# One position of the second convolution filtered along columns, a two-chunk map between the convolutions, and inner column sums in pairs

## The chip, the cores and the metric

The kernel runs on one core of a Trainium2 chip. The metric is the device time of one launch, in microseconds. Engines are named as in the profile: PE multiplies matrices (its weight loads are PEld), DVE, ACT and POOL work on vectors, SP and POOL issue DMAs. "L1482" is line 1482 of the kernel before.

## The reference

Four layers on an image batch x of 4 x 256 x 56 x 56 in float32, each with a group norm in front and a residual around it:

```python
x = x + involution_7x7(gn(x), ...)            # layer 0
x = x + basic_block(gn(x), w1, ..., w2, ...)  # layer 1: the one that changes
x = x + involution_7x7_bn(gn(x), ...)         # layer 2
x = x + fourier_gate(gn(x), W, b)             # layer 3

def basic_block(x, w1, ..., w2, ...):
    h = relu(bn1(conv3x3(x, w1)))
    return relu(x + bn2(conv3x3(h, w2)))      # 256 channels in and out
```

## The kernel before

**Layer 1 as a whole.** `conv_layer` (L1183) holds both convolutions. An image is cut into three chunks of rows, so that there are 12 chunks over the 4 images: for the first convolution `C1_ROWS` (20, 18 and 18 rows), for the second `C2_ROWS` (16, 20 and 20 rows). The list `order` (L1682) alternates them: first convolution of chunk 0, then, for i from 1 to 11, first convolution of chunk i and second convolution of chunk i-1, and last the second convolution of chunk 11. One entry of `order` is called a step here.

**Six positions.** Each row of 56 pixels is 14 tiles of four. `transform` (L1382, DVE) turns the 3-tap filtering along a row into six positions k, in the order `KS = (1, 2, 3, 4, 0, 5)`; `row_weights` and `summed_weights` make six weight planes of them for each of the three filter rows. For one position, PE multiplies 128 x 128 weight blocks with columns of n*14 pixels, n being the rows of the chunk, and DVE and ACT join the six products to four output pixels.

**Two ways to do a position.** `unfiltered` (L1478) takes the three filter rows as they are: for each of two output halves, two input halves times three filter rows, so 12 matmuls of n*14 columns, all on L1482. The filtered way, which stands inside `conv1` (L1510 to L1537), also filters along columns: it takes pairs of rows, and does with four products what six did. That is 16 matmuls of n/2*14 columns, on L1520. It needs prepared inputs: two inner sums (L1464, L1465, on DVE) and an outer difference v[y]-v[y+2]. The difference is two instructions (L1457 and L1458): ACT writes the negated lower rows, and a POOL DMA adds the upper rows onto it. In chunk 1 alone DVE makes it (L1455). It also needs prepared weights (`column_weights`, `filter_weights`) and more joining: ACT copies the first inner product (L1529), DVE forms its difference and sum with the second (L1533, L1534) and adds the outer products (L1536). The first convolution uses the filtered way in all six positions from chunk 2 on, in five in chunk 1 and in none in chunk 0. The second convolution uses `unfiltered` everywhere.

**A matmul in float32 is two records** of PE in this profile, each with its own weight load: a step with 72 unfiltered matmuls shows 144 records.

**Order of the work around them.** Program order on each engine is written out by hand. Each step has lists `after[0]` to `after[11]`, two for each position, that `run_all` empties at fixed points between the matmuls; they hold the transforms of the chunks to come, the column sums (`columns`, L1443), the scaled input rows (`phases`, L1363), loads, and what the step before left over (`tail1`, `tail2`, `late_r`). PSUM is four buffers of two banks: a filtered position takes two buffers, an unfiltered one takes one, so that PE must wait when DVE or ACT has not read the products from two filtered positions ago.

**The map between the convolutions.** `ph2` holds a whole image of the first convolution's result, 58 rows with the edges; `input2` transforms from it 18, 20 and 20 new rows for the three chunks, and copies two known rows for the second and third.

**The end of a second-convolution chunk.** Position 0 and position 5 are done by output half: position 0 half 0, position 5 half 0, position 0 half 1, position 5 half 1 (L1656 to L1670), with `joined` after each half. In the last two chunks `joined` adds the residual on DVE (L1611, L1616), from one shared buffer `res` that ACT fills (L1587); in the others ACT writes (L1603) and a POOL DMA accumulates the residual.

Of the kernel before, what the change touches and what calls it, by code (L numbers as in the profile page):

```python
# [16 lines left out]
P = 128  # L17
# [38 lines left out]
C1_ROWS = [(0, 20), (20, 38), (38, 56)]  # L56
# [16 lines left out]
def net_kernel(  # L73
# [1109 lines left out]
    def conv_layer(xin, xout, st, ahead):  # L1183
        with ExitStack() as es:
# [51 lines left out]
            v2_sb = wpool.tile([P, 2 * NY], F32, name="v2_sb")  # L1236

            def new_v2(half):

                n_v2[half] += 1  # L1240
                at = (n_v2[half] - 1) % 4
                if half:
                    return [room["v2"][:, at * NY : (at + 1) * NY]]
                if at == 3:
                    return [room[r][:, 5 * NY : 5 * NY + NY // 2] for r in ("v2", "xr")]
                t = room["v2"][:, 4 * NY : 5 * NY] if at == 2 else v2_sb[:, at * NY : (at + 1) * NY]
                return [t[:, : NY // 2], t[:, NY // 2 :]]
# [63 lines left out]
            def column_weights(ci, k0, k1):  # L1311

                w0, w1, w2 = (u1_sb[:, ci, y, k0:k1, :] for y in range(3))
                x = between_weights(ci, k0, k1)
                s = y_tile(5 if k0 == 5 else 3)[:, : (k1 - k0) * C].rearrange("p (k n) -> p k n", n=C)
                tt(s, w0, w2, ALU.add)
                tt(x, s, w1, ALU.subtract)
                tt(w1, s, w1, ALU.add)


            PL, VP = (0, 2, 1, 3), (0, 1, 2, 3, 5, 4)
            ph1 = wpool.tile([P, 4, CV_ROWS + 2, NB, WT + 1], F32, name="ph1")
            ph2 = wpool.tile([P, 4, H + 2, NB, WT + 1], F32, name="ph2")
# [3 lines left out]
            for j in range(4):  # L1327
                for y in (0, H + 1):
                    nc.gpsimd.memset(ph2[:, j, y], 0.0)
# [33 lines left out]
            def phases(i):  # L1363

                y0, y1, lo, hi = rows1(i)
                n, r0, known = y1 - y0 + 2, lo - (y0 - 1), 2 if i % 3 else 0
# [5 lines left out]
                for ci in range(NB):  # L1372
                    at = ci * (CV_ROWS + 2) * W
                    xr = room["rows"][:, at + known * W : at + (hi - lo) * W].rearrange("p (r t j) -> p j r t", t=WT, j=4)
                    for j in range(4):
                        q, t0 = (j + 1) % 4, (j + 1) // 4
                        dst = ph1[:, PL[q], r0 + known : r0 + hi - lo, ci, t0 : t0 + WT]
# [4 lines left out]
            def transform(v, ph, y0, n, known):  # L1382

                if known is not None:
                    old, m = known
                    nc.scalar.copy(
                        v[:, :, : 2 * NB].rearrange("p k r t -> p k (r t)"),
                        old[:, :, m * NB : (m + 2) * NB].rearrange("p k r t -> p k (r t)"),
                    )
                    v, y0, n = v[:, :, 2 * NB :], y0 + 2, n - 2  # L1390
# [36 lines left out]
            v_sb = [wpool.tile([P, WPOS, (CV_ROWS + 2) * NB, WT], F32, name=f"v{k}") for k in range(2)]  # L1427

            def input1(i):
                y0, y1, _, _ = rows1(i)  # L1430
                v = v_of[1, i] = v_sb[min(i, 1)]
                p0, p1 = C1_ROWS[i % 3 - 1]
                known = (v_of[1, i - 1], p1 - p0) if i % 3 else None
                yield from transform(v, ph1, 0, y1 - y0 + 2, known)

            def input2(i):
                y0, y1 = C2_ROWS[i % 3]
                v = v_of[2, i] = v_sb[i == n_chunks - 1]
                p0, p1 = C2_ROWS[i % 3 - 1]
                known = (v_of[2, i - 1], p1 - p0) if i % 3 else None  # L1440
                yield from transform(v, ph2, y0, y1 - y0 + 2, known)

            def columns(i, k, half):  # L1443

                y0, y1, _, _ = rows1(i)
                n = y1 - y0
                m = n // 2
                v = v_of[1, i][:, VP[k]]
                if half:
                    (t,) = new_v2(1)  # L1450
                    v = v.rearrange("p r t -> p (r t)")
                    at = slice(0, n * NB * WT)
                    below = slice(2 * NB * WT, (n + 2) * NB * WT)
                    if i == 1:
                        tt(t[:, at], v[:, at], v[:, below], ALU.subtract)  # L1455
                    else:
                        nc.scalar.mul(t[:, at], v[:, below], -1.0)  # L1457
                        nc.gpsimd.dma_start(t[:, at], v[:, at], accum_op=ALU.add)  # L1458
                    t = t.rearrange("p (r e n) -> p e r n", e=2, n=NB * WT)
                    v2_of[i, k, 1] = [t[:, e] for e in range(2)]  # L1460
                else:
                    v = v.rearrange("p (r e c) t -> p e r (c t)", e=2, c=NB)
                    t = v2_of[i, k, 0] = [x.rearrange("p (r n) -> p r n", n=NB * WT) for x in new_v2(0)]
                    tt(t[0][:, :m], v[:, 1, :m], v[:, 0, 1 : m + 1], ALU.add)  # L1464
                    tt(t[1][:, :m], v[:, 0, 1 : m + 1], v[:, 1, :m], ALU.subtract)  # L1465


            FIRST = [(k, half) for k in KS[:4] for half in range(2)]
# [16 lines left out]

            def conv1(i, after, tail):
# [3 lines left out]
                m = n // 2 * WT  # L1490
                a, t, b, s, q = (y_tile(k)[:, : NB * n * WT] for k in (0, 1, 2, 5, 4))
                first = s if i else q
                home = {1: s, 2: q, 3: t, 4: s, 0: y_tile(3)[:, : NB * n * WT], 5: s}

                def outputs(*js):
                    for j in js:
                        o = (a, t, b, q)[j].rearrange("p (c r t) -> p c r t", c=NB, t=WT)
                        p, t0 = PL[(j + 1) % 4], (j + 1) // 4
                        for co in range(NB):
                            nc.scalar.activation(  # L1500
                                ph2[:, p, y0 + 1 : y1 + 1, co, t0 : t0 + WT],
# [7 lines left out]
                for n_s, k in enumerate(KS):  # L1509
                    if k in filtered(i):  # L1510
                        va = v2_of[i, k, 0]
                        vb = v2_of[i, k, 1]
# [372 lines left out]
```

## Time and profile before

| | before |
|---|---|
| median of three runs | 1740.52 us (1738.83 to 1744.15) |
| the profiled execution, its own time | 1735.74 us |
| its span, first to last instruction | 1733.9 us |
| granted PE clock, mean over the span | 0.984 |
| PE busy, weight loads busy | 96%, 85% of the span |
| DVE, ACT, POOL busy | 76%, 54%, 27% of the span |
| layer 1 on PE, first to last convolution matmul | 517.9 to 1186.3 us |
| L1482, unfiltered | 1896 records, 422.8 us |
| L1520, filtered | 2080 records over all its groups |

The durations of single PE records overlap, since matmuls are pipelined: how long a matmul takes in a stream is read from the distance of the starts. A timeline row gives the start, the length, the engine, line and shape, the number of merged instructions, and in brackets the idle time before it with what ended it. A windows row gives, for one stretch, each engine's busy time with the number of instructions in brackets, then the granted clock, the DMA share and the data rate.

### The profile page before, as it was taken

What the parts mean: (1) busy time and instruction counts of PE and PEld (TensorE: products, weight loads), DVE (VectorE), ACT (ScalarE), POOL (GpSimd) and SP (SyncE); (2) the same over time, 40 slices, a digit from 0 to 9 for tenths busy, and PEclk for the clock granted to TensorE, in tenths of its full rate; (3) what the DMA queues carried; (4) which work ended last, traced back from release to release, by engine and by line L of the source; (5) the groups of instructions that cost most, each with busy time, mean ns of one, the idle gap of its engine ahead of it and who ended that gap; (6) DMA issues with size and microseconds to landing.
All of it is one profiled execution on the core that took longest, in us unless ns stands there. A gap on an engine that the chain in (4) does not pass through costs nothing.

```text
span 1733.9 us, 56359 instructions
## 1 busy us (share of the span) xinstructions
PE 1664.7 (96%) x24296; PEld 1479.3 (85%) x24296; DVE 1317.1 (76%) x2467; ACT 933.5 (54%) x2024; POOL 476.4 (27%) x669
## 2 busy tenths in 40 slices
PE   6999999999999999999999999998999899999998
PEld 4998998888977999898899889986988788788886
DVE  2777787777769887798878888856787678778775
ACT  2655556456646455443455245325667567577564
POOL 2223322323334111211122111100000563563571
PEclk9999999999989999999999999999999999999996
DMA  2455444543659546454565354553444666664652
GB/s 89 129 167 162 137 151 160 166 129 103 220 184 260 95 106 142 76 125 96 119 143 97 82 118 92 100 167 104 147 142 151 206 208 196 210 209 161 203 161 103
DMA packets 89030, 252.15 MB, mean 145 GB/s; under 512 B 14453, under 2 KB 35966, under 8 KB 85070
## 3 DMA queue, kind: packets, MB, share of 16 engines
q1 hardware_dynamic: 57438, 163.33, 29.1%
q0 software_dynamic: 30304, 83.95, 22.6%
q8 instruction: 192, 3.15, 0.8%
q10 hardware_dynamic: 1040, 1.26, 0.3%
q14 instruction: 56, 0.46, 0.1%
HBM read 95.07 MB, written 49.15 MB: 83 GB/s over the span
## 4 chain that ended last, share of the span: by engine, by line
PE 70%; DVE 15%; DMA 4%; ACT 4%; issue 3%; SPq 2%; POOL 2%; ACTq 0%; POOLq 0%; DVEq 0%
PE mm L1482 22%; PE ps L593 14%; PE ps L635 14%; PE mm L1520 11%; DVE kt L611 5%; PE ps L407 3%; DVE un L655 3%; DMA xw<-xw 2%; DMA u_sb<-in_wc_dram 2%; PE ps L469 2%; DVE st L1105 1%; ACT hp L488 1%; SPq L425 1%; ACT kt L604 1%; PE ps L718 1%
## 5 line engine op out<-in xcount | busy, mean ns | idle before, releaser
L1482 PE MATMUL mm<-v,u_sb 128*128 128x280 f32 (+2 forms) x1896 | 422.8, 384 | 0.7 <-DVE xs L1534 0.7
L1482 PEld LDWEIGHTS mm<-v,u_sb 128*128 128x128 f32 x1896 | 357.8, 189 | 62.2 <-issue 1.7
L635 PE MATMUL ps<-kt,xw 126*32 126x48 f32 (+1 forms) x12544 | 378.9, 235 | 20.9 <-issue 8.2
L635 PEld LDWEIGHTS ps<-kt,xw 126*32 126x32 f32 (+1 forms) x12544 | 340.6, 121 | 65.8 <-issue 41.5
L593 PE MATMUL ps<-hp,z_sb 64*126 64x133 f32 x6144 | 385.2, 279 | 9.2 <-DVE kt L611 5.0
L593 PEld LDWEIGHTS ps<-hp,z_sb 64*126 64x126 f32 x6144 | 365.1, 186 | 25.7 <-DVE kt L611 7.1
L611 DVE TENSOR_TENSOR kt<-ps,zb_sb 126x798 f32<-126x798 f32 x352 | 333.0, 980 | 59.4 <-PE ps L593 59.0
L604 ACT ACTIVATE kt<-ps,zb_sb 126x133 f32<-126x133 f32 x960 | 281.0, 442 | 108.4 <-PE ps L593 108.4
L655 DVE SCALAR_TENSOR_TENSOR un<-ps,s,un 128x240 f32<-128x240 f32 x224 | 102.4, 457 | 83.4 <-ACT un L650 79.3
L1520 PE MATMUL mm<-xs,u_sb 128*128 128x126 f32 (+1 forms) x1296 | 159.7, 277 | 4.4 <-DVE xs L1534 2.6
L655 DVE SCALAR_TENSOR_TENSOR un<-ps,par_sb,un 128x240 f32<-128x240 f32 x224 | 97.5, 456 | 82.0 <-ACT un L648 78.1
L1520 PEld LDWEIGHTS mm<-xs,u_sb 128*128 128x128 f32 x1296 | 153.3, 191 | 5.4 <-issue 2.9
L660 POOL TENSOR_TENSOR xs<-un,xs 128x240 f32<-128x240 f32 x112 | 72.1, 665 | 216.1 <-DVE un L655 216.1
L419 ACT COPY xw<-ps 126x896 f32<-126x896 f32 x112 | 101.4, 906 | 41.7 <-DMA xw<-xw 22.8
L1458 POOL DMA_DIRECT2D xs<-v x60 | 52.8, 1015 | 249.4 <-ACT xs L1457 248.5
L407 PE MATMUL ps<-ident_sb,strip_sb 128*126 128x128 f32 x784 | 111.6, 282 | 7.7 <-issue 4.3
L150 POOL TENSOR_TENSOR norm_sb<-norm_sb,mhalf 128x1 f32<-128x1 f32 x32 | 19.2, 601 | 360.5 <-DVE norm_sb L149 360.5
L648 ACT ACTIVATE un<-ps,par_sb 128x240 f32<-128x240 f32 x112 | 50.3, 449 | 119.4 <-PE ps L635 109.8
L650 ACT ACTIVATE un<-ps,bn_t,s 128x240 f32<-128x240 f32 x112 | 60.2, 538 | 88.2 <-PE ps L635 80.0
L407 PEld LDWEIGHTS ps<-ident_sb,strip_sb 128*126 128x126 f32 x784 | 84.2, 140 | 19.5 <-issue 5.4
L1603 ACT ACTIVATE xs<-hp,raw,raw 128x1120 f32<-128x1120 f32 (+1 forms) x20 | 45.2, 2260 | 97.7 <-DVE hp L1666 97.7
L1379 ACT ACTIVATE ph<-xs,norm_sb 128x294 f32<-128x294 f32 (+2 forms) x96 | 80.7, 865 | 9.5 <-DMA xs<-x 7.6
(291 smaller groups left out, 2010.0 us busy)
## 6 DMA issues: line engine op xcount, KB each, us to landing
xw<-xw SPq DMA_DIRECT2D x224, 252.0 KB
xw<-xw SPq DMA_DIRECT2D x224, 126.0 KB
xs<-x POOLq DMA_DIRECT2D x26, 560.0 KB, 5.9
x<-xs POOLq DMA_DIRECT2D x8, 1568.0 KB, 8.2
xs<-x SPq DMA_DIRECT2D x8, 1568.0 KB
xs<-v POOLq DMA_DIRECT2D x42, 252.0 KB, 4.2
xs<-in_x_dram SPq DMA_DIRECT2D x6, 1568.0 KB
x<-xs SPq DMA_DIRECT2D x6, 1568.0 KB
```

Source lines behind the costliest of these rows:

```text
L407: nc.tensor.transpose(ps[:Q, k * P : (k + 1) * P], flat[:, k * Q : (k + 1) * Q], ident_sb)
L419: nc.scalar.copy(xw[:, :NSB, :], ps[:Q, : NSB * P].rearrange("q (n c) -> q n c", n=NSB))
L593: nc.tensor.matmul(ps[:Q, i, k * NT : (k + 1) * NT], z_sb[i * R : (i + 1) * R, cb * GB // 2 + gp, z0 : z0 + Q], hp[i * R : (i + 1) * R, py ...
L604: nc.scalar.activation(kt[:, g0 + i, pb, :, k], ps[:Q, i, k * NT : (k + 1) * NT], AF.Identity, bias=zb_sb[:, cb * GB + g0 + i, p0 + k : p0 ...
L611: nc.vector.tensor_tensor(kt[:, g0 : g0 + 2, pb], ps[:Q, :, : PB * NT].rearrange("q i (k t) -> q i t k", k=PB), zb_sb[:, cb * GB + g0 : cb ...
L635: nc.tensor.matmul(v[m * j : m * j + m, i, :, k * TP : (k + 1) * TP], xw[:, window(ty), m * j : m * j + m], kt[:, ng * j : ng * j + ng, :, ...
L650: nc.scalar.activation(part, o[0], AF.Identity, bias=bn["t4"][:, cb : cb + 1], scale=bn["s4"][ng][:, 0, cb : cb + 1])
L655: nc.vector.scalar_tensor_tensor(part, o[e], s, part, ALU.mult, ALU.add)
L660: nc.gpsimd.tensor_tensor(dst, u, dst, ALU.add)
L1379: nc.scalar.activation(dst, xr[:, j], AF.Identity, bias=t, scale=s)
L1482: nc.tensor.matmul(ps, *position(u, v, ci, dy, k, co, n), start=(j == 0), stop=(j == NB * 3 - 1))
L1520: nc.tensor.matmul(ps[:, bank, co * m : (co + 1) * m], u[ci][:, co * P : (co + 1) * P], v2[e][:, : n // 2, ci * WT : (ci + 1) * WT], start ...
```

## The change

- **Row split.** The first convolution's chunks are 18, 20 and 18 rows. The second's stay.
- **Position 0 of the second convolution is filtered**, in all 12 chunks. A new function `filtered_product` holds what stood in `conv1`, and both convolutions call it. Its prepared weights (`column_weights2`, `filter_weights2`) are made during the second convolution's chunk 0. `conv2` now does five positions whole, in the order 1, 2, 3, 4, 0, and position 5 by output half.
- **Column sums.** `columns` becomes `inner_columns`, which makes the two inner sums of two positions in one pair of DVE instructions, and `outer_columns`. The pair (0, 5) of the first convolution is made at the head of its own step.
- **Map of two chunks.** `ph2` is two halves of 20 rows, used in turn. `input2` transforms 19, 20 and 19 new rows, and copies three known ones. POOL clears the one edge row of a chunk (`edge_rows`).
- **Buffers and places.** The inner sums of positions 1 and 2 lie in two planes of `ph1`, and `phases` of the next chunk therefore starts at `after[4]` and not at `after[1]`. The outer differences have five buffers. In the last two chunks each output half has its own residual buffer. The ACT and POOL part of the second half's `joined` moves into the next step, and its store one step later.

```diff
-C1_ROWS = [(0, 20), (20, 38), (38, 56)]
+C1_ROWS = [(0, 18), (18, 38), (38, 56)]
+PH_ROWS = 20
...
+            FILTERED2 = (0,)
+            ux2_sb = [wpool.tile([P, NB, C], F32, name=f"ux2_{k}") for k in FILTERED2]
+            def column_weights2(ci, k):
+                s = y_tile(5)[:, :C]
+                column_sums_of(*(u2_sb[:, ci, y, k, :] for y in range(3)), ux2_sb[FILTERED2.index(k)][:, ci], s)
...
-            ph2 = wpool.tile([P, 4, H + 2, NB, WT + 1], F32, name="ph2")
+            ph2 = wpool.tile([P, 4, 2 * PH_ROWS, NB, WT + 1], F32, name="ph2")
...
+            def inner_columns(conv, i, *ks):
+                n = rows_of(conv, i)
                 m = n // 2
...
+                t = t[:, : len(ks)].rearrange("p k e (r n) -> p k e r n", n=NB * WT)
+                tt(t[:, :, 0, :m], v[:, :, 1, :m], v[:, :, 0, 1 : m + 1], ALU.add)
+                tt(t[:, :, 1, :m], v[:, :, 0, 1 : m + 1], v[:, :, 1, :m], ALU.subtract)
+            def outer_columns(conv, i, k):
...
+                if (conv, i) == (1, 1):
+                    tt(t[:, at], v[:, at], v[:, below], ALU.subtract)
+                else:
+                    nc.scalar.mul(t[:, at], v[:, below], -1.0)
+                    nc.gpsimd.dma_start(t[:, at], v[:, at], accum_op=ALU.add)
...
-                res = ux_sb.rearrange("p c k n -> p (c k n)")[:, : n * W]
+                results = [u1_sb[:, co].rearrange("p y k n -> p (y k n)")[:, : n * W] for co in range(NB)]
...
+                        def leaves():
+                            nc.scalar.activation(x.rearrange("p (q j) -> p j q", j=4), y, AF.Identity, bias=t, scale=s)
+                            nc.gpsimd.dma_start(x, xin[bb][co][:, at], accum_op=ALU.add)
+                        if co == 0:
+                            leaves()
+                        else:
+                            late_r[0].append(leaves)
...
-                for n_s, k in enumerate(KS[:4]):
+                for n_s, k in enumerate(KS[:5]):
+                    if n_s == 4:
+                        residual(0)
+                    if k in filtered2(i):
+                        ux = [ux2_sb[FILTERED2.index(k)][:, ci] for ci in range(NB)]
+                        filtered_product(2, i, k, s, u2_sb, ux, after[2 * n_s])
+                        full, got = (lambda x: x), s
+                    else:
...
+                    else:
+                        stt(full(p), full(p), -0.75, got, ALU.mult, ALU.add)
+                        stt(p, r, 0.25, p, ALU.mult, ALU.add)
                     run_all(after[2 * n_s + 1])
-                residual(0)
+                residual(1)
                 for co in range(NB):
                     at = slice(co * m, (co + 1) * m)
                     ps = one_bank()[:, :m]
-                    unfiltered(ps, u2_sb, v, 0, co, n)
-                    stt(p[:, at], p[:, at], -0.75, ps, ALU.mult, ALU.add)
-                    stt(p[:, at], r[:, at], 0.25, p[:, at], ALU.mult, ALU.add)
-                    run_all(after[8 + 2 * co])
-                    ps = one_bank()[:, :m]
                     unfiltered(ps, u2_sb, v, 5, co, n)
...
+                    if i > 0:
+                        after[0].append(lambda i=i: (inner_columns(1, i, 0, 5), outer_columns(1, i, 0)))
+                        if i > 1:
+                            after[2].append(lambda i=i: outer_columns(1, i, 5))
...
-                            place(after, phases(i + 1), range(1, 10))
+                            place(after, phases(i + 1), range(4, 12))
...
+                    if filtered2(i):
+                        after[2].append(lambda i=i: inner_columns(2, i, *filtered2(i)))
+                        for n, k in enumerate(filtered2(i)):
+                            after[2 + n].append(lambda i=i, k=k: outer_columns(2, i, k))
...
-                        for n, (k, half) in enumerate(FIRST):
-                            after[(5, 5, 6, 6, 7, 7, 8, 8)[n]].append(lambda j=j, k=k, half=half: columns(j, k, half))
+                        columns_at(after, (6, 8), ((4, 1), (4, 2), (6, 3), (9, 4)), 1, j)
```

## Prediction

> **What bounds the kernel now.** First the page's busy shares, then the two stretches of layer 1 in the windows view:
>
> ```profile
> PE 1664.7 (96%) x24296; PEld 1479.3 (85%) x24296; DVE 1317.1 (76%) x2467; ACT 933.5 (54%) x2024; POOL 476.4 (27%) x669
> ```
> ```profile
> 517.90:575.30 57.40, 53.36 (x307) 45.86 (x306) 54.05 (x95) 35.01 (x60) 21.46 (x18) 0.99 1.14 242
> 575.30:1186.30 611.00, 608.90 (x3700) 553.05 (x3698) 498.70 (x901) 259.79 (x375) 95.23 (x111) 1.00 0.50 108
> ```
>
> From 575 us to 1186 us PE is busy 608.9 of 611.0 us at full clock. Who kept it waiting there is the whole answer of the waits view for PE (wait in total, times, longest):
>
> ```profile
> PE mm L1520 <- DVE xs L1534: 1.1, 2, 0.5
> PE mm L1482 <- DVE xs L1534: 0.7, 3, 0.2
> ```
>
> So PE bounds this stretch, and a PE microsecond saved is an end moved, as long as the others keep up. The first 57 us are different: DVE is busy 54.05 of 57.40 us, more than PE, and PE waits for it 4.1 us.
>
> What a matmul costs in a stream I read from the starts in PE's timeline:
>
> ```profile
> 663.29 1.12 PE L1520 MATMUL mm<-xs,u_sb 128*128 128x140 f32 x8
> ...
> 686.17 34.12 PE L1482 MATMUL mm<-v,u_sb 128*128 128x280 f32 x144
> 720.13 1.05 PE L1520 MATMUL mm<-v_sb,u_sb 128*128 128x126 f32 x8
> ...
> 741.57 27.41 PE L1482 MATMUL mm<-v,u_sb 128*128 128x224 f32 x144
> 768.81 1.05 PE L1520 MATMUL mm<-xs,u_sb 128*128 128x126 f32 x8
> ```
>
> Per record: 280 columns (720.13-686.17)/144 = 235.8 ns; 224 columns (768.81-741.57)/144 = 189.2 ns; 140 columns (686.17-663.29)/192 = 119.2 ns; 126 columns (741.57-720.13)/192 = 111.7 ns. The 252-column records take 5.10/24 = 212.5 ns (575.33 to 580.43).
>
> DVE's timeline shows how near the 16-row second-convolution step (741.57 to 768.81 on PE) is to a DVE bound:
>
> ```profile
> 752.86 0.61 DVE L1645 TENSOR_TENSOR hp<-hp,mm 128x448 f32<-128x448 f32 x1
> ...
> 761.51 0.61 DVE L1650 TENSOR_TENSOR hp<-hp,mm 128x448 f32<-128x448 f32 x1
> ```
>
> Four positions of 24 records (4.54 us) put the second product on PE at 750.65 and the fourth at 759.73: DVE reads them 2.2 and 1.8 us late, and works from 741.24 to 767.5 almost without a gap.
>
> [...] 140 columns follow the slope of the longer ones ((235.8-189.2)/56 = 0.83 ns a column), 126 columns lie 4 ns above it. [...] The trace has 0.68 us for 504 and 0.41 for 252, so merging two into one saves. [...] The DMA list of the page has 4.2 us median for this very accumulation; the measurement is used.
>
> **The change, part by part.**
>
> *Position 0 filtered.* 24 records of n*14 columns become 32 of half as many. 20 rows: 24 x 235.8 = 5.66 us against 32 x 119.2 = 3.81 us, 1.85 us saved, in 8 chunks 14.8 us. 16 rows: 24 x 189.2 = 4.54 us against 32 records of 112 columns, which the trace doesn't show. By the slope they would take 96 ns (saving 1.47 us), by the 126-column row[...] 111.7 ns (saving 0.97 us). I take the floor because 126 columns already sit on it: 4 x 0.97 = 3.9 us, upper end 5.9. Sum **-18.7 us**.
>
> *What it adds on DVE*, per 16-row step, in start-to-start time: inner sums 2 x 0.31; joining 0.38 + 0.38 + 0.57; position 0 in two whole instructions (1.2) for four halves (1.5); the four pairs of 252 (8 x 0.33) become two pairs of 504 (4 x 0.60), -0.25; 19 transformed rows for 18, +0.2. Together +1.6 us. DVE needed some 26.2 us of 27.2; now 27.8 us of 26.3. It ends that step 1.5 us behind, perhaps 2. Does PE feel it? Behind it comes a first-convolution step of 21.4 us in which DVE has 17.6 busy (windows view, 720.1 to 741.6), and PE needs a PSUM buffer only two positions after it filled it: the inner one is read some 1 us after the inner half (1.79 us) and due again at 7.14 us, over 3 us of slack. So **0**; if the cover is gone, 1.5 us in 4 steps. 20-row steps have 27.7 us of DVE busy in 33.9 us and go to about 29.2 in 32.1 (686.2 to 720.1).
>
> *ACT and POOL*: per chunk one negation (L1457, 0.62 us), one copy (0.38 us) and one DMA issue (0.87 us); ACT is busy 260 of 611 us, POOL 95. The difference is issued about 8 us into the step, behind the transform it reads, and lands 4 to 5 us later; PE needs it at 4 x 4.54 + 1.79 = 20 us (16 rows) or 24 us (20 rows). **0**. Behind the negation stand ACT's copies of positions 3 and 0, needed at 13.6 us at the earliest. The moved half of `joined` (ACT 2.0 to 2.5 us) now stands behind the first copy of the next step instead of in front; in the trace that copy made DVE wait 1.47 us (724.00) without a PE wait, so **0** again. Its POOL DMA comes ahead of the difference for position 0 of the first convolution, due 14 us later. Its store passes to SP behind the next row loads, which are needed a step later.
>
> *Row split and start.* Chunk 0 loses 144 x (235.8-212.5) = 3.4 us on PE, chunk 1 gains 160 x (119.2-111.7) + 24 x 23.3 ns = 1.7 us. Were PE the bound, -1.7 us. But this stretch is DVE's. Its work up to PE's last wait (566.3 us): chunk 0's transform -0.8, its joining 10 x -0.06 = -0.6, chunk 1's transform +0.7, column sums +0.9 (20 rows, and position 5's, which isn't used there): +0.2. It begins 0.4 us earlier, as ACT's eight `phases` have 19 rows for 21. Behind that wait PE still has 80 filtered records and 24 others, now longer by 80 x 7.5 + 24 x 23.3 ns = 1.2 us. A `phases` instruction of 0.7 us that stood ahead of ACT's copy there has moved to a later slot: -0.7. **+0.3 us**, bounds -1.7 and +2. The second convolution's chunk 0 also gets six DVE instructions of 0.42 us for the weights; it had 3.9 us of DVE gaps (580 to 608): 0. Later images have the same three sizes in another order: 0.
>
> *The tail.* The chain of waits from 1180 us:
>
> ```profile
> 1181.66 1.40 DVE ux_sb L1611
> 1183.08 2.20 DVE xs L1616
> 1185.31 2.41 ACT ux_sb L1587
> 1187.74 1.40 DVE ux_sb L1611
> 1189.16 2.29 DVE xs L1616
> ...
> 1191.74 0.84 POOL strip_sb L371
> ```
>
> Layer 2 starts behind the second L1616, 5.2 us after PE's end (1186.25). With two residual buffers ACT's 2.41 us leave this chain, but half 0 is now complete only 2.83 us before PE's end, not 5.66. DVE then runs (0.46 + 0.48 + 1.40 + 2.20) twice, with gaps 9.2 us, from 2.8 before the end to 6.4 after: **+1.2 us**, bounds 0 and 1.5.
>
> Sum: -18.7 + 0.3 + 1.2 = **-17.2 us**. The profiled execution took 1735.74 us, with 1733.9 of span: it becomes 1718.5. The median shown, 1740.52, lies 4.8 us above that execution; the same step from it gives **1723 us**.
>
> **The rivals.**
> - *DVE becomes the bound of the second-convolution steps.* For it: the lag of 2 us in the 16-row step. Against it: PSUM slack, and no PE wait above 0.5 us in 611. If the 4 x 1.5 us pass on and the 8 steps of 20 rows stall by half a us each: 1723 + 6 + 4 = 1733.
> - *PE gets all of it.* 112 columns stream at 96 ns (-2.0), the start follows PE (-2.0), the tail is hidden (-1.2): 1718.
> - *Slower: the outer difference lands late.* One place, the outer matmuls of position 0: the matmuls queued behind them on PE would stop too, in every chunk. DMA is busy in the first 5 us of such a step with loads and stores. Each us beyond the due time costs 12 us; the gain is gone at 1.4 us late. That needs 13 to 16 us from issue to landing; the page has 4.2 to 5.3. At 2 us late: 1747.
> - *The change doesn't do what it says*: excluded, since 32 records of half the width stand in place of 24 in each chunk of the program.
>
> **How the numbers follow.** Main case 0.64, PE gets all 0.14, DVE bound 0.15, late difference 0.04, gains lost in waits that I don't see 0.03 (about the time before). Within 0.3% (5 us, about what a measurement of this kernel can tell from no change) are only part of the DVE case and the last. Faster 0.90, same 0.05, slower 0.05. Range: from the second rival less 2 us for the spread of the runs, 1716, to the DVE case, 1733.
>
> **What would show it.** Right: L1540 in place of L1520 with 2464 records, 32 of them in 3.81 us in 20-row chunks and 3.57 in 16-row ones; second-convolution steps of 26.3 and 32.1 us on PE; PE waits after 580 us still about 2 us. Wrong: waits of L1540 for DVE or for `xs` DMAs at position 0, first-convolution steps longer than 21.5 and 22.9 us, or a first filtered chunk that ends later than 581.5 us.

## The result and the profile after

Median before 1739.84 us (1738.83 to 1744.15, 4 runs), after 1723.64 us (1722.16 to 1725.63, 4 runs): ratio 0.9903, 95% interval 0.9888 to 0.9917. That is 16.2 us less. The forecast was 1723, counted from 1740.52, the median of the three runs before that were known then. The profiled execution took 1723.6 us, with a span of 1721.7.

First the busy shares on the page, then the windows view for the two stretches of layer 1 (one from the start of its convolutions to the end of the filtered matmuls of the first convolution's chunk 1, and one from there to the last convolution matmul):

```profile
PE 1646.4 (96%) x24392; PEld 1472.2 (86%) x24392; DVE 1331.7 (77%) x2445; ACT 945.0 (55%) x2054; POOL 486.7 (28%) x681
```
```profile
519.70:577.05 57.35, 52.77 (x307) 48.78 (x306) 55.29 (x90) 33.17 (x57) 21.46 (x18) 0.96 1.14 241
577.05:1171.90 594.85, 590.66 (x3796) 543.49 (x3794) 513.92 (x881) 274.97 (x408) 107.26 (x130) 1.00 0.55 116
```

PE has 96 records more (8 in each of 12 chunks) and 18.3 us less to do; DVE has 15 us more, in fewer instructions. The second stretch, 611.0 us long before, is 594.85 us: the gain lies there. It is smaller than PE's busy time fell, so PE waits longer than it did. In the kernel after, L1525 is the line of the unfiltered matmuls and L1540 that of the filtered ones; L1551 is the sum that was L1534. PE's waits after 575 us (wait in total, times, longest):

```profile
PE mm L1540 <- DVE xs L1551: 3.0, 1, 3.0
PE ps L448 <- DVE hp L1725: 2.3, 1, 2.3
PE mm L1525 <- DVE xs L1551: 1.1, 3, 0.4
```

The second line is behind the last convolution. The third is of a kind that was there before (0.7 us in three waits, L1482 for L1534). The first, 3.0 us in one piece, is new, and most of what follows is about it.

The filtered product itself, in PE's timeline, in a chunk of 20 rows and in one of 16:

```profile
706.86 1.12 PE L1540 MATMUL mm<-v_sb,u_sb 128*128 128x140 f32 x8
707.81 1.12 PE L1540 MATMUL mm<-v_sb,ux 128*128 128x140 f32 x8
708.77 2.07 PE L1540 MATMUL mm<-xs,u_sb 128*128 128x140 f32 x16
710.67 5.82 PE L1525 MATMUL mm<-v,u_sb 128*128 128x280 f32 x24
...
757.37 1.04 PE L1540 MATMUL mm<-v_sb,u_sb 128*128 128x112 f32 x8
758.25 1.06 PE L1540 MATMUL mm<-v_sb,ux 128*128 128x112 f32 x8
759.14 1.95 PE L1540 MATMUL mm<-xs,u_sb 128*128 128x112 f32 x16
760.93 4.72 PE L1525 MATMUL mm<-v,u_sb 128*128 128x224 f32 x24
```

From start to start: 32 records of 140 columns take 3.81 us, 32 records of 112 columns 3.56 us (111.3 ns each).

**Where layer 1 got its time.** I cut it into three stages: *start* (from the first matmuls of layer 1 to the end of the first convolution's chunk 1), *convolutions* (from there to the last convolution matmul) and *tail* (from there to layer 2's first activation). Two small matmuls, 0.1 us, lie between the first two stages. Below are the stages of every profiled execution in this study, in us.

| kernel | start | convolutions | tail | layer 1 |
|---|---|---|---|---|
| before | 67.2 | 605.7 | 6.8 | 679.8 |
| after | 67.7 | 589.0 | 8.0 | 664.8 |
| after, again (e5) | 67.3 | 589.8 | 8.0 | 665.2 |
| e1, position 0 not filtered | 67.4 | 604.1 | 8.0 | 679.7 |
| e2, DVE makes chunk 11's difference | 67.5 | 585.8 | 8.1 | 661.6 |
| e3, five sets of inner sums | 67.5 | 601.7 | 8.0 | 677.3 |
| e4, row split of before | 68.7 | 589.6 | 7.9 | 666.3 |
| e6, half 0 of the tail on ACT and POOL | 67.5 | 590.1 | 8.8 | 666.5 |
| e7, three edits | 67.1 | 585.8 | 9.0 | 662.0 |
| e8, two positions filtered | 66.7 | 587.7 | 10.3 | 664.8 |
| e9, two edits | 66.7 | 585.9 | 8.1 | 660.9 |
| e10, store on SP | 69.0 | 585.9 | 8.1 | 663.2 |

The layers around it are the same code in all of them, and yet what lies ahead of these stages took 513.2 to 519.6 us, and what lies behind them 534.8 to 541.8 us. A single execution says little about 3 us, then. The convolution stage repeats within a us (589.0, 589.8), so that the experiments are read from the stages first, and from the medians as a check.

One thing must be known for reading the table. The windows view shows PE's clock granted in full in most of layer 1 (1.00 over the second stretch of after), but in places at 0.50, mostly for 3.4 us at a time and close behind a wait of PE (in after from 558.7 to 562.1 us, behind a wait of 2.69 us that ended at 557.88). Where nothing hides a piece of 3.4 us, it costs some 1.7 us (in e4, below, 5.30 us for 3.57). In the convolutions there are two of them in e3, three in e8 and one each in e5 and e6, and none in the others. In the start of e4 and e10 there is one that nothing hides.

Layer 1 fell by 15.0 us in the profiled pair. The layers ahead of it were 1.8 us longer in that execution of after and those behind it 1.0 us: span 12.2 us shorter.

### The profile page after: what moved, and what is told of

Read it like the earlier page. It is cut to its first block, busy times and chain, and to the rows that moved or that the text cites. A ratio compares the mean times of both kernels' runs of the same rounds, so it can differ in the third digit from the quotient of the medians.

```text
span 1721.7 us, 56615 instructions
## 1 busy us (share of the span) xinstructions
PE 1646.4 (96%) x24392; PEld 1472.2 (86%) x24392; DVE 1331.7 (77%) x2445; ACT 945.0 (55%) x2054; POOL 486.7 (28%) x681
## 4 chain that ended last, share of the span: by engine, by line
PE 61%; DVE 22%; DMA 5%; issue 5%; ACT 4%; SPq 2%; POOL 1%; ACTq 0%; DVEq 0%; POOLq 0%
PE ps L594 14%; PE mm L1525 13%; PE ps L636 13%; PE mm L1540 10%; DVE kt L612 6%; DMA xw<-xw 4%; PE ps L408 3%; DVE un L656 3%; PE ps L470 2%; DMA xs<-x 1%; SPq L426 1%; DVE st L1106 1%; ACT hp L489 1%; SPq L427 1%; ACT xw L420 1%
## 5 line engine op out<-in xcount | busy, mean ns | idle before, releaser
L636 PE MATMUL ps<-kt,xw 126*32 126x48 f32 (+1 forms) x12544 | 378.3, 235 | 23.1 <-DMA xw<-xw 11.3
L594 PEld LDWEIGHTS ps<-hp,z_sb 64*126 64x126 f32 x6144 | 365.3, 186 | 25.4 <-DVE kt L612 7.8
L1525 PE MATMUL mm<-v,u_sb 128*128 128x280 f32 (+2 forms) x1608 | 358.9, 383 | 1.1 <-DVE xs L1551 1.1
L1525 PEld LDWEIGHTS mm<-v,u_sb 128*128 128x128 f32 x1608 | 302.8, 189 | 50.1 <-issue 1.2
L1540 PE MATMUL mm<-xs,u_sb 128*128 128x126 f32 (+2 forms) x1216 | 152.2, 278 | 0.0
L1508 POOL DMA_DIRECT2D xs<-v x71 | 65.0, 956 | 288.1 <-ACT xs L1507 266.5
L1540 PEld LDWEIGHTS mm<-xs,u_sb 128*128 128x128 f32 x1216 | 145.8, 191 | 0.0
L151 POOL TENSOR_TENSOR norm_sb<-norm_sb,mhalf 128x1 f32<-128x1 f32 x32 | 19.7, 627 | 343.2 <-DVE norm_sb L150 343.2
L1411 ACT ACTIVATE ph<-xs,norm_sb 128x266 f32<-128x266 f32 (+2 forms) x96 | 80.7, 865 | 9.5 <-DVE u_sb L1274 7.6
L1507 ACT ACTIVATE xs<-v 128x504 f32<-128x504 f32 (+2 forms) x71 | 45.3, 640 | 64.7 <-DVE v L1443 36.8
```

Source lines behind the costliest of these rows:

```text
L594: nc.tensor.matmul(ps[:Q, i, k * NT : (k + 1) * NT], z_sb[i * R : (i + 1) * R, cb * GB // 2 + gp, z0 : z0 + Q], hp[i * R : (i + 1) * R, py ...
L636: nc.tensor.matmul(v[m * j : m * j + m, i, :, k * TP : (k + 1) * TP], xw[:, window(ty), m * j : m * j + m], kt[:, ng * j : ng * j + ng, :, ...
L1411: nc.scalar.activation(dst, xr[:, j], AF.Identity, bias=t, scale=s)
L1525: nc.tensor.matmul(ps, *position(u, v, ci, dy, k, co, n), start=(j == 0), stop=(j == NB * 3 - 1))
L1540: nc.tensor.matmul(ps[:, bank, co * m : (co + 1) * m], u[ci][:, co * P : (co + 1) * P], v2[:, : n // 2, ci * WT : (ci + 1) * WT], start=(c ...
```

## The experiments

**e1: which part brings the gain?** The change without its main part: position 0 of the second convolution stays unfiltered, all else as in after.

```diff
-            FILTERED2 = (0,)
+            FILTERED2 = ()
```

> The changed kernel with position 0 of the second convolution unfiltered again in all 12 chunks, and all its other edits kept. If the whole gain is position 0 (8 x 1.85 + 4 x 0.97 = 18.7 us on PE, less the 3.0 us that PE waits in the last step of the changed kernel), this comes out at 1723.6 + 18.7 - 3.0 = 1739 us, level with the kernel before, and its second-convolution steps take 34.0 and 27.3 us on PE. If the other edits (paired sums, moved instructions, row split) bring part of the gain by themselves, it stays clearly under that, at 1730 us or less.

Measured: 1739.95 us (12 runs), ratio 1.0, interval 0.9983 to 1.0017. The gain is position 0. The other edits (row split, pairs of sums, map of two chunks, residual buffers) come to nothing together, within the 3 us of the interval. By stages: +0.2 in the start, -1.6 in the convolutions, where some waits at the heads of steps went, and +1.3 in the tail.

**e2: what is PE waiting for in the last step?** The last step is the second convolution of chunk 11. POOL's queue there in after (start, length, in brackets the idle time before it and what ended it):

```profile
1143.48 0.86 POOL L1681 DMA_DIRECT2D xs<-x  x1 [29.82 <-ACT xs L1680]
1149.90 0.57 POOL L1682 DMA_DIRECT2D x<-xs  x1 [5.55 <-DMA xs<-x]
1150.48 0.87 POOL L1681 DMA_DIRECT2D xs<-x  x1
1159.28 0.55 POOL L1682 DMA_DIRECT2D x<-xs  x1 [7.93 <-DMA xs<-x]
1159.88 0.85 POOL L1508 DMA_DIRECT2D u_sb<-v  x1
```

L1681 and L1682 are the end of chunk 10 (the function `added`): POOL accumulates the residual of each half, waits until that has landed, and stores it. The outer difference of chunk 11 (L1508) stands behind both stores. It goes out 23.5 us after the step began (1136.34), where I had put 8. The list of DMA issues has its way from there to landing, 4.1 us:

```profile
u_sb<-v POOLq DMA_DIRECT2D x1, 280.0 KB, 4.1
```

So it lands at about 1164.0. And on PE:

```profile
1159.06 1.12 PE L1540 MATMUL mm<-v_sb,u_sb 128*128 128x140 f32 x8
1160.01 1.12 PE L1540 MATMUL mm<-v_sb,ux 128*128 128x140 f32 x8
1164.10 2.15 PE L1540 MATMUL mm<-u_sb 128*128 128x140 f32 x16 [2.97 <-DVE xs L1551]
```

The bracket names DVE's L1551, which also ended at 1164.0. Two theories, then: the late transfer, or DVE's joining (it was held up by the same accumulation, 8.0 us, at 1159.01). The edit lets DVE make the difference of chunk 11 in one instruction; L1551 stays where it was.

```diff
-                if (conv, i) == (1, 1):
+                if (conv, i) in ((1, 1), (2, n_chunks - 1)):
```

> In the last second-convolution step alone DVE makes the outer difference in one instruction, in place of ACT and a POOL DMA. Theory: PE's 2.97 us wait there is for this DMA, which stands on POOL behind the residual transfers of chunk 10 and was issued at 1159.9 us, so the wait goes and the time falls by some 3 us, to 1720.7. Rival: the wait is for L1551, which the profile names, since DVE was held for 8.0 us by statistics that need the same residual transfer; then the wait stays at about 3 us and the time at 1723.6.

Measured: 1719.53 us (5 runs), ratio 0.9884 (0.9864 to 0.9903). The convolution stage is 585.8 us for 589.0, 3.2 us less. In e2 the outer products start at 1163.27 without a wait, and L1551 ends at 1166.10, 2.8 us later. The transfer held PE, not L1551.

**e3: how much slack has DVE?** My theory gave the 16-row steps over 3 us of it. The edit makes the inner sums of position 0 five times: 2.9 us more for DVE in each step of 20 rows, 2.5 us in each of 16, 33 us in all, with nothing else changed.

```diff
-                        after[2].append(lambda i=i: inner_columns(2, i, *filtered2(i)))
+                        after[2] += [lambda i=i: inner_columns(2, i, *filtered2(i))] * 5
```

> The inner sums of position 0 in the second convolution are made five times over: 8 more DVE instructions of 0.31 to 0.36 us in each of 12 steps, 2.5 to 2.9 us a step and 33 us in all. Theory: DVE's lag is taken up by the PSUM buffers and by the first-convolution steps, so the time moves by less than 3 us. Rival: DVE is already the bound of the second-convolution steps; then it passes on, 10 us at least (the 16-row steps alone) and up to 33 us.

Measured: 1730.8 us (6 runs), ratio 0.9946 (0.9928 to 0.9965); convolutions 601.7 us, +12.7 on after. The profiled execution (1733.69 us) is the slowest of the six. The steps of 20 rows hid nearly all of their 2.9 us: on PE their three parts still take 22.64, 3.81 and 5.66 us. In the 16-row steps nearly all of the 2.5 us came through. PE's timeline of e3 around one of them, position 5 of the step and the head of the next second-convolution step:

```profile
762.91 2.45 PE L1525 MATMUL mm<-v,u_sb 128*128 128x224 f32 x12
765.99 2.51 PE L1525 MATMUL mm<-v,u_sb 128*128 128x224 f32 x12 [0.62 <-DVE hp L1713]
768.33 1.05 PE L1540 MATMUL mm<-ph,u_sb 128*128 128x126 f32 x8
...
792.21 1.18 PE L1525 MATMUL mm<-v,u_sb 128*128 128x280 f32 x4 [1.93 <-DVE xs L1551]
```

Position 5 took 5.42 us for 4.56, and the first-convolution step behind it 23.88 us for 22.28: 2.46 of 2.5 us. The next two such steps passed on 2.42 and 2.43 us. Another 1.1 us came through in chunk 0, 0.6 behind steps of 20 rows and 0.3 in the last step, which makes 9.3 us. The other 3.4 us are PE's clock and not DVE's work directly: behind a wait of 1.92 us ahead of chunk 10's step and one of 3.25 us in the last step, the granted clock was 0.50 from 1115.0 to 1118.4 and from 1176.4 to 1179.8, and the matmuls there took 1.7 us longer each time. My theory of over 3 us of slack fell: once the change is in, the 16-row steps have next to none left.

**e4: is the row split worth anything?** The rows of before, with everything else of the change.

```diff
-C1_ROWS = [(0, 18), (18, 38), (38, 56)]
-PH_ROWS = 20
+C1_ROWS = [(0, 20), (20, 38), (38, 56)]
+PH_ROWS = 21
...
-ph1 = wpool.tile([P, 4, PH_ROWS, NB, WT + 1], F32, name="ph1")
+ph1 = wpool.tile([P, 4, CV_ROWS + 2, NB, WT + 1], F32, name="ph1")
...
-v, ph2, i % 2 * PH_ROWS, (19, 20, 19)[i % 3], v_of.get((2, i - 1)), p1 - p0, known_rows(i, 3)
+v, ph2, i % 2 * PH_ROWS, (21, 18, 19)[i % 3], v_of.get((2, i - 1)), p1 - p0, (0, 5, 3)[i % 3]
```

> The changed kernel with the row split of before (20, 18 and 18 rows for the first convolution; the second transforms 21, 18 and 19 rows, and the map has 21 rows a half). Theory: the start is bound by DVE, and the split does next to nothing: within 1.5 us of the changed kernel. Rival: PE bounds the start too, so that the new split had saved 1.7 us, and this is 1.7 us slower or more.

Measured: 1719.86 us (6 runs), ratio 0.9892 (0.987 to 0.9913), no slower than after. The profiled execution has 68.7 us in the start, 1.0 more than after. That is PE's clock and not the split. The windows view of e4 has 3.4 us at half clock, and PE's timeline shows what they cost, right behind PE's last wait of the start:

```profile
566.20:569.60 3.40, 3.40 (x18) 3.40 (x18) 3.05 (x7) 0.85 (x3) 1.52 (x2) 0.50 1.24 197
```
```profile
565.58 1.54 PE L1540 MATMUL mm<-v_sb,u_sb 128*128 128x126 f32 x8 [2.89 <-DVE xs L1553]
...
570.88 1.06 PE L1540 MATMUL mm<-v_sb,u_sb 128*128 128x126 f32 x8
...
574.45 1.05 PE L1540 MATMUL mm<-v_sb,u_sb 128*128 128x126 f32 x8
```

The 32 records of one position took 5.30 us there and 3.57 us in the next. e10, whose start is that of after, had the same piece at the same place (567.4 to 570.8) and 69.0 us; after had it ahead of PE's last wait (558.7 to 562.1). With 1.7 us taken off, an estimate from these figures, the starts are 67.0 us in e4 and 67.3 in e10; six other executions with the start of after had 67.3 to 67.7. So the split brings nothing that can be seen here, and not the 1.7 us that PE alone would give.

**e5: after again**, for a size of the spread between chips and executions.

> The changed kernel once more, on the chip of the three that follow. Both theories expect 1723.6 us within 3 us; its stretches in layer 1 (67.7 us from the warm-up matmuls to the end of chunk 1, 589.0 us to the last convolution matmul, 8.0 us to layer 2's first activation) should come back to within 0.5 us, while layers 0 and 2 may differ by some us from run to run.

Measured: 1725.86 us (4 runs), ratio 0.9901 (0.9871 to 0.9931). The stages are in the table. The wait in the last step is there again, and in this trace it is put down to the transfer itself:

```profile
1167.36 2.97 PE L1540 MATMUL mm<-u_sb 128*128 128x140 f32 x16 [2.13 <-DMA u_sb<-v]
```

It is shorter here, but the clock granted behind it was 0.50 from 1168.5 to 1171.9. Wait and clock together cost 4.0 us against a last step without either (e7).

**e6: can the tail be shortened?** In after the tail hangs on DVE, which the chain of waits shows from the last matmuls on (start, length, what):

```profile
1166.24 2.84 PE mm L1525 x12
...
1169.11 0.46 DVE hp L1725
...
1170.08 1.40 DVE u_sb L1666
...
1171.50 2.17 DVE xs L1671
1173.66 0.36 DVE hp L1725
...
1174.61 1.40 DVE u_sb L1666
```

Both halves now stand on DVE almost without a break, and ACT's 2.41 us, which stood in this chain before, are gone. The edit gives the end of half 0 to ACT and POOL:

```diff
                     if i == n_chunks - 1:
-                        stt(xj, rj, 0.0, xj, ALU.max, ALU.add)
+                        if co == 0:
+                            nc.scalar.activation(rj, rj, AF.Relu)
+                            nc.gpsimd.tensor_tensor(xj, rj, xj, ALU.add)
+                        else:
+                            stt(xj, rj, 0.0, xj, ALU.max, ALU.add)
```

> In the last chunk the relu and the add of the residual of half 0 leave DVE: ACT does the relu, POOL the add; half 1 stays as it is. Theory: the tail is DVE's chain of both halves, so half 1 starts at PE's end and not 1.6 us behind it, and the stretch from the last convolution matmul to layer 2's first activation falls from 8.0 to about 6.4 us. Rival: it is PE's wait for its PSUM buffers or POOL's memset that holds layer 2, and the stretch stays at 8.0 us.

Measured: 1727.1 us (6 runs), ratio 0.9909 (0.988 to 0.9937); the tail took 8.8 us, longer than the 8.0 of after. A miss. DVE did get to the second half earlier, but look at its timeline in e6 (the line after it is POOL's):

```profile
1174.12 1.39 DVE L1666 SCALAR_TENSOR_TENSOR u_sb<-hp,s,u_sb 128x1120 f32<-128x1120 f32 x1
...
1177.02 4.07 DVE L1666 SCALAR_TENSOR_TENSOR u_sb<-hp,s,u_sb 128x1120 f32<-128x1120 f32 x1
```
```profile
1176.75 3.17 POOL L1673 TENSOR_TENSOR xs<-u_sb,xs 128x1120 f32<-128x1120 f32 x1 [12.55 <-ACT u_sb L1672]
```

The same instruction takes 1.39 us alone and 4.07 us when POOL's addition started 0.27 us ahead of it; POOL's ends at 1179.92 and DVE's at 1181.09. So DVE lost 2.7 us in 2.9 us that the two ran together; whether it stood or ran slower, the trace doesn't show. e7 and e8 have the same tail. There another DVE instruction, L1675, took 5.02 and 5.00 us for the 2.19 us of e6, where it started behind the end of POOL's addition: in e7 and e8 it started 1.0 and 0.7 us behind the end of ACT's relu (L1672), which POOL's addition follows by 0.1 us in e6. I had not reckoned with it. Without the 2.7 us the tail of e6 would have been 6.2 us, by an estimate from these figures, near the 6.4 expected.

**e7: three edits together**: that of e2, that of e6, and one at the start, where the sums of position 5 are made for chunk 1 and never used.

```diff
-after[0].append(lambda i=i: (inner_columns(1, i, 0, 5), outer_columns(1, i, 0)))
+after[0].append(lambda i=i: (inner_columns(1, i, *((0, 5) if i > 1 else (0,))), outer_columns(1, i, 0)))
```

> Three repairs at once: the difference of the last chunk on DVE, the tail of e6, and chunk 1 of the first convolution without the inner sums of position 5, which it doesn't use. Theory (start bound by DVE, last step by the late DMA, tail by DVE): 0.7 us at the start, 3.2 us in the last step and 1.6 us at the tail, so 5.5 us under the changed kernel on the same chip, 1718 us. Rival: the start is held by transfers of weights and not by DVE; then the start stays as it is, and 4.8 us are gained.

Measured: 1718.7 us (4 runs), ratio 0.9866 (0.9833 to 0.9898), 7.2 us below after in the same batch (e5) by the medians, 3.2 us by layer 1. The convolutions gain 4.0 on e5 (2.3 us of wait and 1.7 us of clock), the start 0.2, the tail loses 1.0.

**e8: a second position, on top of e7.** If PE were still the bound, position 4 should bring as much as position 0.

```diff
-            FILTERED2 = (0,)
+            FILTERED2 = (4, 0)
```

> e7 with position 4 of the second convolution filtered as well. On PE that is another 8 x 1.85 + 4 x 0.97 = 18.7 us less; on DVE about 2 us more in each second-convolution step. Theory, after e3: the 20-row steps have DVE to spare for 2 us, the 16-row steps have none and pass on all of it. So 8 x 1.85 = 14.8 us less and 4 x (2.0 - 0) = 8 us more, 7 us under e7, about 1711 us. Rival: with PE shorter too, DVE bounds the 20-row steps as well, and the time is that of e7 or above.

Measured: 1724.36 us (4 runs), ratio 0.9897 (0.9866 to 0.9927): 5.7 us above e7, 2.8 us by layer 1. The first two of PE's waits after 575 us in e8:

```profile
PE mm L1525 <- DVE xs L1551: 7.5, 6, 1.9
PE mm L1540 <- DVE xs L1551: 2.6, 3, 1.9
```

PE waits for joining in every 16-row step and behind it. The steps of 20 rows gain 1.85 us where nothing waits (30.3 us on PE for 32.1), those of 16 rows gain nothing (26.2 to 26.4 for 26.3, and 29.4 in chunk 0), and the first-convolution steps behind them take 24.5 us for 22.3 (chunk 0: 23.1 for 21.4). Three pieces at half clock behind such waits add to it. That is the rival "DVE becomes the bound", one position later than I had priced it.

**e9: the two edits that helped**, without the tail's.

```diff
-                if (conv, i) == (1, 1):
+                if (conv, i) in ((1, 1), (2, n_chunks - 1)):
...
-after[0].append(lambda i=i: (inner_columns(1, i, 0, 5), outer_columns(1, i, 0)))
+after[0].append(lambda i=i: (inner_columns(1, i, *((0, 5) if i > 1 else (0,))), outer_columns(1, i, 0)))
```

> The two edits that have shown a gain, without the third: the outer difference of position 0 in chunk 11 is made by DVE in one instruction, and position 5's inner sums are not made for chunk 1 of the first convolution, where they aren't used. The instructions at the end of layer 1 are those of the changed kernel. Expected from the stages: 67.1 us for the start of layer 1 (as with all three edits), 585.8 us for the two convolutions (as with the DVE edit), 8.0 us for the tail (as in the changed kernel, for 9.0 with the edited tail): 660.9 us for layer 1, 3.9 us below the changed kernel's 664.8. So the median should lie 4 us below that of the changed kernel, about 1719.5, ratio 0.988, and about 1 us below the kernel with all three edits where the untouched layers take as long. If the tail's edit had helped and something else lengthened that stage, the tail would come out at 9 us or more here.

Measured: 1718.37 us (6 runs), ratio 0.9862 (0.9837 to 0.9888). Stages 66.7, 585.9 and 8.1 us: layer 1 is the shortest of the study, 3.9 us below after, as expected in sum (1.0 of it in the start and 3.1 in the convolutions, where 0.6 and 3.2 were expected).

**e10: is it the queue or the transfer?** e2 took the transfer away; it doesn't say why it was late. Here it stays on ACT and POOL, and only chunk 10's store leaves POOL's queue.

```diff
                     nc.scalar.activation(xj, rj, AF.Relu)
                     nc.gpsimd.dma_start(x, xin[bb][co][:, at], accum_op=ALU.add)
-                    nc.gpsimd.dma_start(xout[bb][co][:, at], x)
+                    nc.sync.dma_start(xout[bb][co][:, at], x)
```

> One word is changed: the store behind the residual accumulation of chunk 10 (two transfers) is issued by SP and not by POOL. ACT and POOL still make the outer difference of chunk 11. If the queue is what makes it late (POOL cannot issue it, since the store ahead of it waits for the accumulation to land), POOL issues it at about 1151 us of the span and not at 1159.9, it lands before its due time of 1161.1, and the wait of 3.0 us in the last step goes: convolutions 585.8 to 586.3 us for 589.0, median 3 us below that of the changed kernel. If the transfers themselves are what is slow there (the accumulation took 8.5 us), the difference queues behind it in the DMA engines too and lands between 1161 and 1163: 1 us gained or less. If the wait is for DVE after all (its last join before the outer products ends at 1164.0, held up by the same accumulation), nothing is gained: 589.

Measured: 1718.11 us (6 runs), ratio 0.9857 (0.983 to 0.9883); convolutions 585.9 us. POOL's queue in e10, then PE, then DVE:

```profile
1146.41 0.86 POOL L1681 DMA_DIRECT2D xs<-x  x1 [29.82 <-ACT xs L1680]
1148.42 0.86 POOL L1681 DMA_DIRECT2D xs<-x  x1 [1.15 <-ACT xs L1680]
1149.45 0.86 POOL L1508 DMA_DIRECT2D u_sb<-v  x1 [0.17 <-issue]
```
```profile
1162.95 1.12 PE L1540 MATMUL mm<-v_sb,ux 128*128 128x140 f32 x8
1163.90 2.07 PE L1540 MATMUL mm<-u_sb 128*128 128x140 f32 x16
```
```profile
1166.29 0.45 DVE L1551 TENSOR_TENSOR xs<-xs,mm 128x280 f32<-128x280 f32 x1
```

The difference goes out 10.2 us after the step's start (1139.27) in place of 23.5. It now takes 7.8 us to land, behind the accumulation:

```profile
u_sb<-v POOLq DMA_DIRECT2D x1, 280.0 KB, 7.8
```

It is there in time all the same: the outer products follow without a gap. They start 2.8 us before L1551 ends, so that this instruction can't have been what they waited for in after. The cause is the queue: in after the store waited 7.93 us for the accumulation ahead of it to land, and held what POOL had behind it.

## Why the prediction was right, point by point

**Position 0, -18.7 us: right.** 3.81 us in 20-row chunks (predicted 3.81) and 3.56 us in 16-row ones (3.57), in every chunk but the last. 1.85 x 8 + 0.98 x 4 is 18.7. The floor that I chose for 112 columns is there: 111.3 ns a record, as 126 columns had 111.7, and not the 96 ns of the slope. That 112 columns come no faster than 126 was my estimate from the 126-column row; what sets that time, no run here shows.

**DVE's lag, +1.6 us, hidden: the cost was right, the cover was too large.** Between the last join of one step and that of the next, DVE's work rose from 24.0 us (with 1.5 us idle beside it) to 25.4 us (with none): +1.4 us. In the 16-row step shown above DVE's last join ends 2.2 us behind PE, a little over what I gave; before, the same join ended 1.0 us behind. First before, then after:

```profile
769.43 0.39 DVE L1666 SCALAR_TENSOR_TENSOR hp<-hp 128x224 f32<-128x224 f32 x1
```
```profile
766.19 0.38 DVE L1725 SCALAR_TENSOR_TENSOR hp<-hp,mm 128x224 f32<-128x224 f32 x1
...
767.33 0.39 DVE L1726 SCALAR_TENSOR_TENSOR hp<-hp 128x224 f32<-128x224 f32 x1
```

PE's next step had begun at 768.81 before and at 765.49 after, and PE felt 0.1 us of it: 22.28 us for the 22.17 that the same step took before. But "over 3 us of slack" is wrong. e3 added 2.5 us and 2.46 of them came through. I had reckoned with the first PSUM buffer that PE wants back; DVE's lag also goes on to the joining of position 5, and to the end of the first-convolution step behind it, where DVE has little room to recover it. The room that I gave for that step, 17.6 us busy of 21.4, I had read at a step behind 20 rows; behind 16 rows DVE was busy 18.7 of 22.2 us before, and 19.7 of 22.3 us after. The change uses up this cover, and e8 shows what the next step of the kind costs.

**ACT, POOL and the outer difference, 0: right in 11 chunks, wrong in one.** In the ordinary steps it is issued as I said (7.6 us into the step at 739.21, by POOL at 746.83) and waited for nowhere. In the last step, I had taken the same 8 us. There POOL has `added` of chunk 10 ahead of it, and I had not followed its queue, though the trace of before shows it:

```profile
1164.94 0.56 POOL L1627 DMA_DIRECT2D x<-xs  x1 [6.03 <-DMA xs<-x]
```

There the second store held POOL until 12.9 us into the last step (which began at 1152.04), with nothing behind it that mattered. The change itself pushes this back by 10 us, as ACT's timeline of after shows:

```profile
1138.63 2.40 ACT L1633 ACTIVATE u_sb<-xs,shift,norm_sb 128x1120 f32<-128x1120 f32 x1 [9.63 <-DMA xs<-x]
1140.93 4.25 ACT L1680 ACTIVATE xs<-u_sb 128x1120 f32<-128x1120 f32 x2
```

DVE completes half 0 of chunk 10 at 1135.70, 0.6 us ahead of the last step; before it was 3.4 us. And L1680, the first instruction of `added`, now stands on ACT behind the residual of half 1 (L1633, through `residual(1)`, which the change moved ahead of position 5), and that waits for a load until 1138.63. So the first accumulation goes out 7.1 us into the last step, for 0.8 us ahead of it before, and the second store holds POOL until 22.9 us.

Why that load comes so late, SP's queue shows, first its timeline and then its waits:

```profile
1114.00 16.82 SPq L296 DMA_DIRECT2D xs<-x  x2
...
1130.99 32.58 SPq L1392 DMA_DIRECT2D xs<-x  x3
```
```profile
SPq L296 <- PE mm L1540: 13.1, 1, 13.1
```

L1392 at 1130.99 is the load of half 1's residual. Ahead of it stand two loads for layer 2 (L296), into buffers that held outer differences until then, and the second of them waits 13.1 us for PE's filtered matmuls of chunk 10. In e1, which keeps the order of `residual` and leaves position 0 unfiltered, no such wait occurs: the same load goes out 16.5 us into chunk 10's step for 27.2 us in after, and the second store holds POOL until 15.9 us into the last step. So of the 10 us some 3 go with the other edits and some 7 with filtering position 0, by way of this second queue. No run moves that load alone.

So the slower rival's mechanism did occur, 3.0 us late, but in one step and not in twelve: **3.2 us** lost (e2: 589.0 to 585.8). This is the term that the sum lacks.

**Waits at the heads of the first-convolution steps: not in the sum, 1.2 us gained.** Before, ten such steps took 223.4 us in all, after 222.2 us: two of them had been 1.25 us longer than others of their size, of which the waits view puts 0.5 us each on DVE. I had not foreseen this. My mark for them (21.5 and 22.9 us) was badly set, too: before, the step behind each 16-row one already took 22.17 us.

**Row split and start, +0.3 us: right in size.** 67.2 us before, 67.7 and 67.3 us after. The split itself brings nothing that can be seen (e4). That DVE bounds this stretch fits e7, e8 and e9, where DVE has 0.6 us less to do there and the start takes 66.7 to 67.1 us. My mark of 581.5 us for the end of chunk 1 was missed (582.7), but only because layer 0 took 1.8 us longer in that execution: it should have been given from the start of layer 1.

**The tail, +1.2 us: right.** 6.8 us before, 8.0 us after, in the eight executions with this tail 7.9 to 8.1 us, and by the chain that I had worked out.

**The sum.** -17.2 was predicted for layer 1, and -15.0 was measured: -18.7 + 0.5 + 1.2 + 3.2 - 1.2. The profiled execution was to take 1718.5 us and took 1723.6; 2.2 us of that are the missed wait less the unforeseen gain (with 0.2 at the start), 2.8 us are layers that the change doesn't touch. The median agrees to 0.6 us, partly by luck: of 17.2 us it shows 16.2, where layer 1 gained 15.0, over untouched layers that move by several us from run to run.

**The rivals.** DVE as the bound came about only with more work for it (e3, e8). The late difference came in one step of twelve. PE did not get all: the floor, the start and the tail held as in the main case.

## What to carry to other kernels

A DMA that is cheap in every ordinary step must be followed through its queue in the first and the last step too: in after a store that waited 7.93 us for an earlier transfer held what POOL was to issue behind it, and moving that store to another queue (e10) or the work to another engine (e2) was worth 3 us on top of the 16 gained. The same held on SP, where a load for the next layer waited 13.1 us and kept a residual back. Slack that one change uses is gone for the next: before adding the same again, measure the cover with idle copies of the work (e3), stage by stage. When a wait bracket names an instruction that ended together with a transfer, take one of the two away and see. Read the granted clock of each stretch before two executions are compared: in e3 and e4 it made 3.4 and 1.7 us that would otherwise be put down to the edit's work.

## What the runs showed of the hardware

- A DVE instruction of 1.39 us took 4.07 us when a POOL addition of 3.17 us, also on 128x1120 float32, had started 0.27 us ahead of it (e6); one of 2.19 us took 5.02 and 5.00 us when it started 1.0 and 0.7 us behind the relu that the same addition of POOL follows (e7, e8). In e6 what ACT and POOL took over was one DVE instruction of 2.17 us (after), and DVE lost 2.7 us.
- An accumulating transfer of 280 KB took 4.1 us from issue to landing when the accumulations ahead of it had landed (after), and 7.8 us when issued 1.0 us behind one of 560 KB (e10).
- Float32 matmul records came 111.3 ns apart in a stream at 112 columns (after) and 111.7 ns apart at 126 (before), where 0.83 ns a column, from the records of 224 and 280 columns (before), would give 96 ns and 108 ns by estimate.
- The clock granted to PE was 0.50 for 3.4 us behind some waits of PE of 1.9 to 3.3 us (e3, e4, e5, e10) and not behind others: in after it stayed at 1.00 behind the wait of 3.0 us. 32 float32 matmul records of 126 columns took 5.30 us with such a piece and 3.57 us without (e4).
